# Which engine issues the store DMAs of an adaLN transformer block on one core

## The chip, the cores and the metric

One of the eight cores of a Trainium2 chip runs the whole program, in float32. The metric is device time in microseconds, the median of several executions. Beside it there is the profile of one execution of the same program, with every instruction's start, duration and what ended the idle time before it.

## What is computed

The input is four sequences of 1024 tokens of 512 features. A small product gives six modulation vectors for each sequence; the two gates are kept at least 0.25 in size.

```python
mod = (_silu(L0_c) @ L0_wmod).reshape(L0_c.shape[0], 6, 1, -1)
sa, ca, ga, sb, cb, gb = (mod[:, 0], ..., mod[:, 5])
h = _layernorm(x) * (1 + ca) + sa
x = x + ga * attn(h)      # 16 query heads of 32, one key and value head, causal, softmax, output product
h = _layernorm(x) * (1 + cb) + sb
x = x + gb * ffn(h)       # Hadamard transform, up and gate 512 -> 2048, silu(gate) * up,
                          # Hadamard transform, down 2048 -> 512
```

## The kernel before, in words

**Tiling.** The 4096 tokens are eight blocks of 512 (`order`), each of two halves of 256 columns or four tiles of 128 rows. For each block there is attention (scores, row minima, exponentials, scales, transposes, the product with the values), then the feed-forward part: for each of 16 chunks of 128 hidden features the products of gate and up (`gate_up`, products at L1076, arranged so that 14 small products and some sums replace 16), and the products with the transformed down weights (`down`, L1214). Attention of later blocks is mixed on TensorE with the feed-forward part of earlier ones.

**Who sets the order.** The instructions are not written in the order in which they run. Some thirty generators (`ranked`, L1257) yield `Op`s, each with an engine, an estimated cost, the keys that it reads and writes, and the code that emits it. `Flow` (L47) keeps an estimated time for each engine and for the transfers, and emits next the operation that could begin first; among those of the same engine within `SLACK` the stream's rank decides. Each engine then runs its own instructions strictly in the emitted order, and waits, where it must, at the head of its queue. An operation with another engine or cost can therefore change the order everywhere.

**The DMAs.** All of them come from `load` (L288), which makes an operation of SP with a cost of 0.5 us for the planner. SP's queue holds 1270 of them. The ones that matter here:
- `wd<-wd_d` (L1048): a row of the down weights, into a ring of three buffers, once per down step. `wg`, `wu` (L1018): weights of gate and up, rings of two and three. GpSimd mixes them into three sums, four operations for each chunk (`mixes`, L1040).
- `o_d<-oT` (L659): a half of the attention's rows of a tile. ScalarE copies it from PSUM to `oT` in four copies (L640), the store takes it to DRAM, and four loads bring back its quarters in another arrangement (L661), which GpSimd adds up (L663, L664). Then comes the output product of attention. The first block doesn't take this way, so there are 56 such stores, of 512 KB each.
- `x2_d<-xr` (L720; the profile names this tensor x_d): a tile of the residual after attention. GpSimd adds the attention's part to `xr` (L715, L717), the store follows, and VectorE (statistics at L304) and GpSimd (L310, L311) prepare the second normalization. Then `xr` is overwritten in place: by L315 in the first block, and in the later ones by VectorE's L746 and L748, eighteen GpSimd operations of the Hadamard transform (L754), a transpose, and four small stores `xTf_d<-xr`. The loads `bt<-xTf_d` (L772) bring the result back turned, as the right-hand operand of gate and up. There are 32 stores of `x2_d`; `xo<-x2_d` (L1235) reads them much later.
- `out<-xo` (L1250): a tile of the output. VectorE scales the down product (L1243), GpSimd adds the residual (L1248), the store follows. There are 32.

**Semaphores of DMAs.** Eight semaphores are given to the DMAs in turn, and a DMA that gets one waits for the DMA before it on that semaphore, unless this is known to be done.

Of the kernel before, what the change touches and what calls it, by code (L numbers as in the profile page):

```python
# [19 lines left out]
P = 128  # L20
# [141 lines left out]
def adaln_block(ctx, tc, x_d, small_d, const_d, wmod_d, qwT_d, kwT_d, vwT_d, vb_d, owT_d, ob_d,  # L162
                wdp_d, wupT_d, wgT_d, wdT_d, out_d):
    nc = tc.nc
# [15 lines left out]
    x2_d = dram.tile([B * S, D], F32, name="x2_d")  # L180
# [3 lines left out]
    o_d = dram.tile([2, P, 4, HB], F32, name="o_d")  # L184
# [15 lines left out]
    def token(n):  # L200

        b, t = order[n // NT]
        return b * S + t * TB + n % NT * P

    def new_batch(i):
        return i == 0 or order[i][0] != order[i - 1][0]
# [78 lines left out]
    def until(queue, name):  # L285
        return lambda: bool(queue) or name in over

    def load(mb, dst, src, writes, reads=()):  # L288
        return Op("SP", 0.5, lambda: nc.sync.dma_start(dst, src), reads, writes, mb=mb)  # L289

    def bk(b):
        return ("bank", b)
# [9 lines left out]
    def stats_op(which, n, x, dst, keys, key):  # L302
        def emit():
            nc.vector.bn_stats(bn[which][:, n % 2, :], x)  # L304
            nc.vector.bn_aggr(dst, bn[which][:, n % 2, :])
        return Op("DVE", 0.85, emit, keys, [key])

    def rstd_op(dst, src, keys, key):
        def emit():
            nc.gpsimd.tensor_scalar_add(dst, src, EPS)  # L310
            nc.gpsimd.tensor_tensor(dst, dst, mhalf[:, 0:dst.shape[-1]], ALU.pow)  # L311
        return Op("POOL", 1.0, emit, keys, [key])

    def norm_op(x, xk, m, rs, rkey):
        return Op("DVE", 0.62, lambda: nc.vector.tensor_scalar(x, x, m, rs, ALU.subtract, ALU.mult), [rkey], [xk])  # L315

    def turn(which, n, x, xk):


        hh, j = divmod(n, 2)  # L320
        dst = xT_d[which][hh].rearrange("(b q) (j a i) -> j a q b i", q=32, j=2, a=4)[j]
        for a, r in enumerate(rows):
            yield load(0.0625, dst[a], x[r, :].rearrange("q (b i) -> q b i", i=32), [("xT", which, n, a)], [xk])

    def turned_back(which, hh, c, dst, key):

        return load(0.25, dst, xT_d[which][hh][c * P:(c + 2) * P, :].rearrange("(c p) n -> p c n", p=P), [key],
                    [("xT", which, n, a) for n in (2 * hh, 2 * hh + 1) for a in range(4)])
# [23 lines left out]
    def first_norms(halves):  # L352
        for hh in halves:
# [5 lines left out]
            for j in range(2):  # L359
                r = token(2 * hh + j)  # L360
                yield load(0.25, x[:, j, :], x_d[r:r + P, :], [(xk, j)])
# [288 lines left out]
    def exchange():  # L650


        while True:
            yield until(to_exchange, "attend")
            if not to_exchange:
                break
            i, ql, half = to_exchange.popleft()
            o, key = oT[:, half], ("oT", half)
            yield load(0.5, o_d[half], o, [("o_d", half)], [key])  # L659
            for j, r in enumerate(rows):  # L660
                yield load(0.125, o[r], o_d[half].rearrange("(c d) j x -> j d c x", c=4)[j], [key], [("o_d", half)])  # L661
            o = o.rearrange("p c x -> p (c x)")
            yield Op("POOL", 1.3, lambda: nc.gpsimd.tensor_add(o[:, 0:512], o[:, 0:512], o[:, 512:1024]), [], [key])  # L663
            yield Op("POOL", 0.77, lambda: nc.gpsimd.tensor_add(  # L664
                aT[:, 2 * half:2 * half + 2, :].rearrange("p c q -> p (c q)"), o[:, 0:HB], o[:, HB:512]), [key], ["aT"])
            st.folded += 1
            to_finish.append((i, ql, half))
        over["exchange"] = True
# [36 lines left out]
    def add():  # L705

        for i in range(NBLK):
            if new_batch(i):
                yield load(0.25, obga, gates_d[2, order[i][0], :].partition_broadcast(P), ["obga"], [("gates", 2)])
            for ql in range(NT):  # L710
                j, n = ql % 2, i * NT + ql
                x, xk, r = xr[:, j, :], ("xr", j), n * P
                yield lambda: st.turned > n - 2
                yield load(0.25, x, x_d[token(n):token(n) + P, :], [xk])
                yield Op("POOL", 1.3, lambda: nc.gpsimd.tensor_add(x, x, obga), ["obga"], [xk])  # L715
                yield lambda: bool(to_add)
                yield Op("POOL", 1.3, lambda: nc.gpsimd.tensor_add(x, x, y), ["y"], [xk])  # L717
                to_add.popleft()
                st.y_held = False
                yield load(0.25, x2_d[r:r + P, :], x, [("x2", n)], [xk])  # L720
                m, rs = mv["f"][:, j, :], rstd["f"][:, j, 0:1]
                yield stats_op("f", n, x, m, [xk], ("mvf", j))
                yield rstd_op(rs, m[:, 1:2], [("mvf", j)], ("rstdf", j))
                if i >= ROWS:
                    to_fwht.append((n, m, rs))
                    continue
                yield norm_op(x, xk, m[:, 0:1], rs, ("rstdf", j))
                st.added = n + 1
# [496 lines left out]
    def outputs():  # L1225
        for hh in range(NHALF):
            i, hf = divmod(hh, 2)
            if hh == 0:
                yield lambda: st.prepared
            if hf == 0 and new_batch(i):  # L1230
                yield load(0.25, ff["gb"], gates_d[1, order[i][0], :].partition_broadcast(P), ["gb"], [("gates", 1)])
            yield lambda: st.normed > i
            for j in range(2):
                n = 2 * hh + j
                yield load(0.25, xo[:, j, :], x2_d[n * P:(n + 1) * P, :], [("xo", j)], [("x2", n)])  # L1235
            yield lambda: bool(to_out)
            _, acc = to_out[0]
            for j in range(2):
                n = 2 * hh + j
                x, xk = xo[:, j, :], ("xo", j)  # L1240
                yield lambda: not st.y_held
                st.y_held = True
                yield Op("DVE", 0.7, lambda: nc.vector.tensor_mul(y, ps[:, acc[j], :], ff["gb"]),  # L1243
                         [bk(acc[j]), "gb"], ["y"])
                banks.give(acc[j])
                if j == 1:
                    to_out.popleft()
                yield Op("POOL", 1.3, lambda: nc.gpsimd.tensor_add(x, x, y), ["y"], [xk])  # L1248
                st.y_held = False
                yield load(0.25, out_d[token(n):token(n) + P, :], x, [("out", n)], [xk])  # L1250


    def early(rank, later):
# [3 lines left out]
    ranked = [  # L1257
        (early(-5.073, -12.067), copies), (early(0.821, 4.686), sums), (early(8.123, -0.319), multiply),
        (early(2.934, -0.393), outputs), (early(6.498, 6.37), load_weights_once), (early(-6.572, -10.863), load_jobs),
        (early(2.446, -2.829), mods), (early(5.09, -0.692), attend), (early(-1.32, 5.096), finish),  # L1260
        (early(0.121, 5.957), exchange), (early(-13.435, 16.471), add), (early(-5.268, 7.992), transformed),
        (early(5.174, 6.804), minima), (early(6.312, -0.74), scores), (early(-13.598, 4.773), second_norms),
        (early(-0.125, 3.627), lambda: first_norms([0])), (early(-5.211, 13.107), lambda: first_norms([1])),
# [60 lines left out]
```

## Time and profile before

| | |
|---|---|
| median of 3 runs | 2028.36 us (2024.61 to 2028.71) |
| the profiled execution, its own time | 2024.31 us |
| its span, first to last instruction | 2022.5 us |
| mean granted clock of TensorE | 0.989 |
| busy on ScalarE, VectorE, GpSimd | 1125.0, 1375.3, 1047.9 us |
| issue to landing, median: o_d<-oT, x_d<-xr, out<-xo | 3.8, 3.1, 2.2 us |

The profile's page lists each engine's busy time (PE is TensorE, PEld its weight loads, DVE VectorE, ACT ScalarE, POOL GpSimd; SP only issues), the chain of work that ended last, the costliest groups of instructions and the DMA issues. A view of the waits gives, for each engine and line, what the wait was for, with the total in us, the number of waits and the longest one. A view by time gives start and duration of each instruction, with the idle time before it and its releaser in brackets. "SPq" is SP's queue: a row there is a DMA's issue, and a wait there holds up all DMAs behind it.

### The profile page before, as it was taken

To read this page: it belongs to the slowest core of one execution; us is meant where nothing else is said; L and a number is where in the kernel's file an instruction comes from. 1 tells how busy PE (TensorE), PEld (TensorE's weight loads), DVE (VectorE), ACT (ScalarE), POOL (GpSimd) and SP (SyncE) were. 2 spreads that over 40 slices of the span, in tenths; PEclk is the share of its full clock that TensorE was granted. 3 is DMA by queue.
4 is the path that set the end of the run, shared out by engine and by line. 5 is a ranking of instruction groups with operands and counts; after the bars stand their busy time and mean duration, and the time that the engine had idled before them with its cause. 6 is when DMAs were issued, how large, how long until landed. Compare 5 with 4: busy or idle time off the path is not lost.

```text
span 2022.5 us, 41770 instructions
## 1 busy us (share of the span) xinstructions
PE 1947.4 (96%) x15656; PEld 1258.1 (62%) x15656; DVE 1375.3 (68%) x3139; ACT 1125.0 (56%) x2371; POOL 1047.9 (52%) x1374
## 2 busy tenths in 40 slices
PE   7898999999999999999999999999999999999998
PEld 5556666556674666746676566663666646674774
DVE  4886778788757667878748688776567768642441
ACT  5677755685557554766546575576455676510220
POOL 2762467636564486447453356444567435662440
PEclk9999999999999999999999999999899999999999
DMA  7433555654347645465345634357554444345333
GB/s 233 135 111 105 161 159 134 184 156 122 107 131 210 178 137 153 136 187 141 103 129 141 199 116 120 101 152 212 149 156 121 131 146 138 104 122 180 107 103 115
DMA packets 387394, 289.42 MB, mean 143 GB/s; under 512 B 129508, under 2 KB 319076, under 8 KB 387192
## 3 DMA queue, kind: packets, MB, share of 16 engines
q1 hardware_dynamic: 387192, 286.75, 49.4%
q8 instruction: 124, 2.03, 0.4%
q14 instruction: 78, 0.64, 0.1%
HBM read 222.67 MB, written 64.00 MB: 142 GB/s over the span
## 4 chain that ended last, share of the span: by engine, by line
PE 85%; DMA 5%; POOL 3%; DVE 3%; issue 3%; SPq 1%; ACT 0%; POOLq 0%; DVEq 0%; ACTq 0%
PE ps L1076 38%; PE ps L1214 19%; PE ps L299 11%; PE ps L626 8%; PE ps L502 7%; DMA wd<-wd_d 2%; SPq L289 1%; DMA xTf_d<-xr 1%; POOL ws L1040 1%; DVE p L526 1%; POOL u L754 1%; DMA wg<-in_wgT 1%; PE ps L984 0%; DMA oT<-o_d 0%; POOL xr L754 0%
## 5 line engine op out<-in xcount | busy, mean ns | idle before, releaser
L1214 PE MATMUL ps<-wd,g 128*128 128x512 f32 x1024 | 485.4, 608 | 24.8 <-DMA wd<-wd_d 19.6
L549 ACT ACTIVATE p<-p,nm 128x512 f32<-128x512 f32 (+7 forms) x512 | 391.2, 768 | 78.5 <-DVE nm L526 78.3
L1076 PE MATMUL ps<-bt,ws 128*128 128x256 f32 x1536 | 380.6, 384 | 5.5 <-DVE bt L807 3.5
L583 ACT ACTIVATE p<-p,rden 128x640 f32<-128x640 f32 (+7 forms) x480 | 347.6, 784 | 46.1 <-DVE rden L563 45.9
L598 DVE STREAM_TRANSPOSE p<-p 128x512 f32<-128x512 f32 (+7 forms) x256 | 342.6, 1359 | 20.8 <-ACT p L583 19.1
L1214 PEld LDWEIGHTS ps<-wd,g 128*128 128x128 f32 x1024 | 187.4, 191 | 256.6 <-issue 189.6
L1076 PEld LDWEIGHTS ps<-bt,ws 128*128 128x128 f32 x1536 | 291.5, 192 | 61.1 <-issue 8.7
L526 DVE CUSTOM_DVE_ANT_0 p<-ps,maskw 128x512 f32<-128x512 f32 (+3 forms) x512 | 279.8, 581 | 53.8 <-PE ps L502 53.6
L1163 DVE TENSOR_TENSOR s<-ps,s 128x256 f32<-128x256 f32 x384 | 160.1, 419 | 198.5 <-PE ps L1076 149.9
L1076 PE MATMUL ps<-bt,wu 128*128 128x256 f32 x1024 | 269.9, 386 | 0.0
L1040 POOL TENSOR_TENSOR ws<-wu 128x256 f32<-128x256 f32 x128 | 105.3, 822 | 285.1 <-DMA wu<-in_wupT 258.3
L1076 PE MATMUL ps<-bt,wg 128*128 128x256 f32 x1024 | 251.2, 383 | 0.9 <-DVE nm L526 0.7
L1076 PEld LDWEIGHTS ps<-bt,wu 128*128 128x128 f32 x1024 | 188.9, 190 | 91.0 <-issue 39.6
L1076 PEld LDWEIGHTS ps<-bt,wg 128*128 128x128 f32 x1024 | 195.0, 192 | 52.4 <-issue 18.2
L626 PE MATMUL ps<-p,vrep 32*32 32x256 f32 (+1 forms) x8256 | 197.3, 410 | 14.7 <-issue 11.5
L754 POOL TENSOR_TENSOR u<-xr 128x256 f32<-128x256 f32 x280 | 171.6, 631 | 48.1 <-DVE xr L748 40.4
L1154 ACT COPY s<-ps 128x256 f32<-128x256 f32 x128 | 47.8, 373 | 245.0 <-PE ps L1076 244.9
L502 PE MATMUL ps<-kT,qT 32*128 32x512 f32 (+3 forms) x1536 | 174.7, 528 | 2.0 <-DVE nm L526 1.2
L1179 ACT ACTIVATE th<-s,wgh 128x512 f32<-128x512 f32 x128 | 92.5, 722 | 147.4 <-DVE s L1163 145.6
L626 PEld LDWEIGHTS ps<-p,vrep 32*32 32x32 f32 x8256 | 120.0, 103 | 85.2 <-issue 38.9
L1040 POOL TENSOR_TENSOR ws<-ws,wg 128x256 f32<-128x256 f32 x128 | 99.7, 779 | 137.0 <-DMA wg<-in_wgT 123.2
L640 ACT COPY oT<-ps 128x256 f32<-128x256 f32 x256 | 78.4, 386 | 126.1 <-PE ps L626 62.7
(118 smaller groups left out, 2317.2 us busy)
## 6 DMA issues: line engine op xcount, KB each, us to landing
wd<-wd_d SPq DMA_DIRECT2D x256, 256.0 KB, 2.9
wg<-in_wgT SPq DMA_DIRECT2D x128, 256.0 KB, 3.5
wu<-in_wupT SPq DMA_DIRECT2D x128, 256.0 KB, 2.8
o_d<-oT SPq DMA_DIRECT2D x56, 512.0 KB, 3.8
oT<-o_d SPq DMA_DIRECT2D x224, 128.0 KB, 3.2
xr<-in_x SPq DMA_DIRECT2D x32, 256.0 KB, 3.4
x_d<-xr SPq DMA_DIRECT2D x32, 256.0 KB, 3.1
xo<-x_d SPq DMA_DIRECT2D x32, 256.0 KB, 3.6
```

The source lines that it names most:

```text
L299: nc.tensor.matmul(out, l, r, start=(k == 0), stop=(k == len(pairs) - 1))
L502: nc.tensor.matmul(ps[:, bb[j], m * n:(m + 1) * n], qT[r, c, u.ql % 2 * P:(u.ql % 2 + 1) * P], kT[r, u.kv[kb] * TB:u.kv[kb] * TB + n], sta ...
L526: yield Op("DVE", 0.245 + 0.00103 * n, lambda: nc.vector.tensor_tensor_reduce(o, ps[:, bb[j], k * n:(k + 1) * n], m, -1.0, nm[:, slot, 0, ...
L549: yield Op("ACT", act_cost(u.kmax) + 0.19, lambda: nc.scalar.activation(e, e, AF.Exp, bias=nm[:, slot, u.t, j:j + 1], scale=-1.0, accum_ou ...
L583: yield Op("ACT", act_cost(u.kmax), lambda: nc.scalar.activation(e, e, AF.Copy, scale=r), [("rden", ds, c)], [u.key(h)])
L598: yield Op("DVE", 0.135 + 0.00105 * 2 * u.kmax, lambda: nc.vector.transpose(e, e), [], [u.key(h), u.key(h + 1)])
L626: nc.tensor.matmul(ps[rows[c], bb[g], 0:w], vrep[rows[g], v0 + c, :], pv[rows[g], :, k:k + 32], start=(kt == 0), stop=(kt == nkt - 1))
L754: yield Op("POOL", 0.66, lambda: getattr(nc.gpsimd, "tensor_" + fn)(w[:, h:h + D // 2], pairs[:, 0, :], pairs[:, 1, :]), [], [xk, "u2"])
L1040: yield Op("POOL", 0.78, lambda: getattr(nc.gpsimd, "tensor_" + e)(a[o][0], a[x][0], a[y][0]), [a[n][1] for n in (x, y) if n != "A21" or o ...
L1076: nc.tensor.matmul(o, w[:, c, :], bt[:, t, c, :], start=start and c == 0, stop=stop and c == 1, skip_group_check=True)
L1163: yield Op("DVE", 0.43, lambda: nc.vector.tensor_add(s[:, j, :], ps[:, bank, half * HB:(half + 1) * HB], s[:, j, :]), [bk(bank)], [sk[j]])
L1214: nc.tensor.matmul(ps[:, acc[j], :], g[:, j * P:(j + 1) * P], ff["wd"][:, m % NWD, :], start=(f == 0), stop=(f == NFC - 1))
```

## The change

`load` is given the issuing engine, SP unless told otherwise. Three stores get another one, the engine that writes the data just before: `o_d<-oT` goes to ScalarE, `x2_d<-xr` and `out<-xo` to GpSimd. The loads stay on SP, and so do the stores `xTa_d`, `xTf_d`, `wd_d` and `gates_d`. The planner counts 0.5 us on the new engine. Lines behind L288 move down by one.

```diff
-    def load(mb, dst, src, writes, reads=()):
-        return Op("SP", 0.5, lambda: nc.sync.dma_start(dst, src), reads, writes, mb=mb)
+    def load(mb, dst, src, writes, reads=(), eng="SP"):
+        issuer = {"SP": nc.sync, "ACT": nc.scalar, "POOL": nc.gpsimd}[eng]
+        return Op(eng, 0.5, lambda: issuer.dma_start(dst, src), reads, writes, mb=mb)
...
             o, key = oT[:, half], ("oT", half)
-            yield load(0.5, o_d[half], o, [("o_d", half)], [key])
+            yield load(0.5, o_d[half], o, [("o_d", half)], [key], "ACT")
...
                 st.y_held = False
-                yield load(0.25, x2_d[r:r + P, :], x, [("x2", n)], [xk])
+                yield load(0.25, x2_d[r:r + P, :], x, [("x2", n)], [xk], "POOL")
...
                 st.y_held = False
-                yield load(0.25, out_d[token(n):token(n) + P, :], x, [("out", n)], [xk])
+                yield load(0.25, out_d[token(n):token(n) + P, :], x, [("out", n)], [xk], "POOL")
```

## The prediction

> **What bounds the kernel now.** I read the page first, then the waits of TensorE, the waits of SP's own queue, and last the timeline of the largest stall that both point to.
>
> ```profile
> span 2022.5 us, 41770 instructions
> PE 1947.4 (96%) x15656; PEld 1258.1 (62%) x15656; DVE 1375.3 (68%) x3139; ACT 1125.0 (56%) x2371; POOL 1047.9 (52%) x1374
> PE 85%; DMA 5%; POOL 3%; DVE 3%; issue 3%; SPq 1%; ACT 0%; POOLq 0%; DVEq 0%; ACTq 0%
> ```
>
> TensorE is the bound: 75 us of the span are not matmul, and no change of issuers removes matmul time. A table by stage (windows) splits the 75: 26 in the first 180 us, about 42 from 180 to 1850, nothing to 1984, 7 in the tail. A gain can come only out of these.
>
> ```profile
> PE ps L1214 <- DMA wd<-wd_d: 19.6, 10, 4.4
> PE ps L626 <- issue: 11.5, 20, 1.1
> PE ps L880 <- DMA raw<-in_wmod: 6.6, 1, 6.6
> PE ps L1214 <- DVE g L1189: 5.2, 9, 0.6
> ```
>
> Of what TensorE waits for, only the first row (us, times, longest) runs through SP: the ring of three down-weight rows.
>
> ```profile
> SPq L289 <- PE ps L1214: 486.9, 223, 9.6
> SPq L289 <- PE ps L1076: 414.8, 204, 10.6
> SPq L289 <- ACT oT L640: 89.1, 20, 8.8
> SPq L289 <- POOL xr L717: 66.9, 15, 16.7
> SPq L289 <- DMA o_d<-oT: 49.0, 25, 5.1
> ...
> SPq L289 <- POOL xo L1248: 39.6, 24, 6.3
> ```
>
> SP mostly waits for TensorE to free weight buffers, which costs nothing. The three moved stores hold it for 89.1 + 66.9 + 39.6 = 196 us. Where that reaches TensorE:
>
> ```profile
> 370.27 0.33 SPq L289 DMA_DIRECT2D x_d<-xr  x1
> 372.35 0.34 SPq L289 DMA_DIRECT2D out<-xo  x1
> 372.78 1.35 SPq L289 DMA_DIRECT2D wd<-wd_d  x3
> ...
> 375.59 1.98 PE L1214 MATMUL ps<-wd,g 128*128 128x512 f32 x4 [3.40 <-DMA wd<-wd_d]
> ```
>
> Three weight loads stand behind two stores that wait for GpSimd's adds, and TensorE stops 3.40 us.
>
> **What is removed from SP.** 120 issues (56 + 32 + 32) at 0.34 to 0.38 us, 44 us, and the 196 us of waiting. The Trainium skill speaks against a gain: "DMA: Bandwidth & Descriptors", section "Issuing engines are not separate DMA queues", says that several issuers save only the sequencer's time to start a DMA. By that rule the gain is the 44 us of an SP that waits over 900 us for TensorE: zero. The rows add what the rule leaves out, in-order blocking, so I count it where TensorE sat idle. The stall above, 3.4 us, goes. Of the other 16.2 us of that row, the timeline shows the two longest (650.8 and 894.9, 4.3 and 4.4 us) behind "bt<-xTf_d" loads that wait for a landing; those stay. The one near 1835 (3.9 us) is a wd load that took 5.5 us to land; no store was waiting in front of it. Gain between 0 and 8 us; I take 4, the proven stall and a little. Much of the 89.1 us doesn't go at all: the quarter loads oT<-o_d stay on SP and must wait for the landing of the same store (49.0 us already), and the order of the programs has only 2.7 SP entries (2.8 after) between a store and its first quarter load. What is late next there is that landing.
>
> **What is added to ScalarE.** 56 issues at 0.38 us, plus an estimated 0.3 us for its own last oT copy to finish: 38 us on an engine idle for 900. It often waits for TensorE anyway (s L1154: 244.9 us, 119 of 128 times). Behind a store in its queue stand exps and the s copies that TensorE's next product needs; if that cover were gone all 38 would show. I take 2, ends 0 and 8.
>
> **A wait that is new.** The built order shows semaphores: 55 of the 56 ScalarE stores also wait on a DMA semaphore, one of eight that all SP and ScalarE DMAs share in turn; for 54 of them the DMA before it on that semaphore is SP's, the eighth before the store. So ScalarE, with exps and s copies behind it, can wait for SP. In the trace SP was the early one: it waited for oT copies 20 times. Stores that follow their copies at once were issued 0 to 2.5 us after the copies ended; eight DMAs back is 8 x 2022/1270 = 13 us earlier on average, and a landing takes about 3. So nothing is to be waited for in most cases, and SP will run further ahead. But weight loads wait for TensorE up to 10.6 us, and a burst of loads after one leaves no margin. Ends: 0, and 10 stores x 8 us, of which TensorE sees half, 40. I take 3, near the zero that the trace speaks for.
>
> **What is added to GpSimd.** 64 stores. No row shows GpSimd issuing a DMA. Nearest rows: an issue on SP, 0.34 us, and a 512-column add on GpSimd, 1.27 us. I take 1.0 each, 64 us on an engine idle for 975 us and waiting 258.3 + 123.2 us for weight loads before its mixes. It shows only where GpSimd's chain sets the end: four x2 stores of the first block (the chain there runs xr L717, p L580, tmp L963, rstdf L310 and L311 from 94.9 to 102.6; TensorE idles 4.1 us at 162 for the normalized row), +3; the 18 GpSimd adds and subtracts per row at later block starts (idle near 1407 to 1424, 5 us), +2; the last output, whose add ends at 2019.5, 3.0 us before the end, +1. Sum +6, ends 0 (at SP's price) and 16.
> The skill has a darker rule: "SBUF — State Buffer", section "SBUF: two separate sides", warns that a DMA issued from GpSimd is starved of descriptors while VectorE holds the shared port, 620 ns becoming about 3100. That would be 2.5 us a store, 160 us on GpSimd, and put this item and the next at their upper ends, +26 together. The trace shows the lock seldom: the add L717 takes 1264/1275/2241 ns min/median/max beside a VectorE that is 68% busy. I follow the row.
>
> **A later landing.** VectorE overwrites xr in place (L746, L315) and waits for the x2 store to have left; now 3.5 us in three waits. If the store lands 0.7 to 1.5 us later, up to 32 x 1 us falls on VectorE, with minima and sums queued behind it. A quarter reaching TensorE: I take 3, ends 0 and 10.
>
> **The order of everything else.** The planner sees other engine loads and reorders. Matmuls, vector and scalar operations are the same set; on TensorE the order first differs at instruction 360 of 7854. Changes between whole-array, row and tile matmuls number 424 before and 420 after. Down steps with under 6 us of matmul since the ring slot was freed: 79 before, 82 after, with 143 and 122 other SP entries ahead of their loads. So the order is as good as before by these counts; 0, ends -8 and +8.
>
> **Sum.** -4 + 2 + 3 + 6 + 3 + 0 = +10 us on the profiled execution's 2024.3 (span 2022.5, 1.8 around it). The median of the runs, 2028.36, is 4 above that execution; I add the 10 there: 2038.
>
> **Rivals.** A measurement tells about 0.2%, 4 us, from no change.
> 1. The sum, costs on GpSimd and ScalarE over a small gain: 2033 to 2054, likeliest 2038. Chance 0.52.
> 2. Faster: with 122 for 143 entries in front of tight weight loads, and none that waits for GpSimd, half of the 19.6 us goes, -9, and GpSimd's issues hide under its 381 us of waiting for weights: about 2020 (2014 to 2024). It decides once a GpSimd store costs no more than SP's 0.34 us, which takes the two GpSimd items from 9 to about 2. For it: the stall at 372; against: the other long stalls aren't behind stores. 0.22.
> 3. It doesn't free SP: the wait for oT reappears as the wait for the store's landing in front of the quarter loads (49 us becoming 120 or more), and GpSimd's price is hidden: 2025 to 2032. 0.14.
> 4. ScalarE waits for SP's semaphore at some ten stores: +40, 2068 (2055 to 2085). 0.12.
> The range 2018 to 2062 leaves out the low end of case 2 and most of case 4. Case 1 alone has 2033 to 2054. Faster 0.22, same 0.14, slower 0.64.
>
> **What would show it.** Right: SP's waits for oT L640, xr L717 and xo L1248 gone, those for DMA o_d<-oT grown; GpSimd rows for stores near 1 us; TensorE's wait for wd under 19.6 us; more idle on TensorE before 180 us; VectorE waits for DMA x_d<-xr above 3.5 us. The semaphore price is wrong if ScalarE rows show waits for SP's DMAs of over 20 us in all. I am wrong altogether if stores on GpSimd cost under 0.4 us (then case 2), or over 2 us (then past 2050).

## The result, and the profile after

The changed kernel takes 2053.48 us (median of 4 runs, 2050.98 to 2059.28) against 2026.48 us for the kernel before beside it: a ratio of 1.0141, 95% interval 1.0111 to 1.0172, so 27 us slower. The forecast was 10 us slower. The profiled execution took 2053.11 us, at nearly the clock of before (0.987 for 0.989).

From the page of the changed kernel: span, busy times and the chain that ended last; from the view of its groups, the two of GpSimd's stores. The groups' columns are busy us and mean ns of one, then the idle time just before.

```profile
span 2051.3 us, 41831 instructions
PE 1958.0 (95%) x15656; PEld 1256.9 (61%) x15656; DVE 1383.2 (67%) x3139; ACT 1125.2 (55%) x2371; POOL 1091.0 (53%) x1438
PE 80%; DMA 6%; issue 4%; POOL 4%; DVE 4%; SPq 1%; ACT 0%; POOLq 0%; DVEq 0%; ACTq 0%
...
L290 POOL DMA_DIRECT2D x_d<-xr x32 | 19.9, 623 | 8.6 <-POOL xr L718 8.6
L290 POOL DMA_DIRECT2D out<-xo x32 | 18.4, 577 | 9.5 <-POOL xo L1249 9.2 <-DMA oT<-o_d 0.3
```

The span grew by 28.8 us. Of that, 10.6 are in the busy row of TensorE (1947.4 to 1958.0, with the same 15656 matmuls; the lower clock alone would make about 4, an estimate from 1947.4 x 0.989/0.987) and 18.2 are idle (75.1 to 93.3). The two groups answer what no row of before could: a store costs GpSimd 0.58 to 0.62 us, and in nearly every case another 0.3 us of waiting for its own add to finish.

The waits of TensorE after (us in total, times, longest):

```profile
PE ps L1215 <- DMA wd<-wd_d: 18.5, 14, 5.1
PE ps L627 <- issue: 14.4, 19, 1.7
PE ps L1215 <- DVE g L1190: 10.8, 16, 2.3
PE ps L881 <- DMA raw<-in_wmod: 6.6, 1, 6.6
PE ps L300 <- ACT aT L687: 3.7, 1, 3.7
```

The wait that the change could have shortened, for down weights, is as long as before (18.5 us for 19.6). The stall at 372 us is gone, and others of the kind stand elsewhere. What grew is spread: 5.6 us more for VectorE's gated product g, 2.9 us in the row "issue", 3.7 us for ScalarE's aT. No new row is near 18 us.

The waits of SP's queue after:

```profile
SPq L290 <- PE ps L1215: 520.9, 220, 9.4
SPq L290 <- PE ps L1077: 477.3, 221, 10.1
SPq L290 <- DVE xr L758: 68.3, 21, 12.8
SPq L290 <- DMA o_d<-oT: 63.9, 21, 10.2
SPq L290 <- DMA out<-xo: 61.4, 25, 6.1
```

And one row of before:

```profile
SPq L289 <- DMA out<-xo: 18.6, 13, 3.3
```

SP no longer waits for xr and xo, and for oT only 8.0 us in three waits. Two things take their place: the wait for the landing of o_d (49.0 to 63.9 us), which the forecast named, and the wait for the landing of out<-xo (18.6 to 61.4 us), which it didn't. The second one stands before the load of the next tile into the same buffer xo. Before, SP waited for xo twice, 39.6 us for the add and 18.6 for the landing, 58.2 together; it now waits 61.4 in one place, so for this store nothing is set free at all. Most of the rest of the time set free is waiting for TensorE: the first two rows hold 998 us, before 902.

The end of the program by time (start, duration, in brackets the idle time before), first before, then after:

```profile
2018.24 1.26 POOL L1248 TENSOR_TENSOR xo<-xo,y 128x512 f32<-128x512 f32 x1 [0.80 <-DVE y L1243]
2019.53 0.34 SPq L289 DMA_DIRECT2D out<-xo  x1
```

```profile
2043.14 1.27 POOL L1249 TENSOR_TENSOR xo<-xo,y 128x512 f32<-128x512 f32 x1
2044.71 0.56 POOL L290 DMA_DIRECT2D out<-xo  x1 [0.30 <-POOL xo L1249]
```

The last add ends at 2044.4 and the span at 2051.3, 6.9 us later. Before, the last add ended at 2019.5 and the span at 2022.5, 3.0 later. So 3.9 us of the loss lie in the tail. The remaining 25 build up gradually over blocks.

### The profile page after: what moved, and what is told of

Read it like the earlier page. It is cut to its first block, busy times and chain, and to the rows that moved or that the text cites. A ratio compares the mean times of both kernels' runs of the same rounds, so it can differ in the third digit from the quotient of the medians.

```text
span 2051.3 us, 41831 instructions
## 1 busy us (share of the span) xinstructions
PE 1958.0 (95%) x15656; PEld 1256.9 (61%) x15656; DVE 1383.2 (67%) x3139; ACT 1125.2 (55%) x2371; POOL 1091.0 (53%) x1438
## 4 chain that ended last, share of the span: by engine, by line
PE 80%; DMA 6%; issue 4%; POOL 4%; DVE 4%; SPq 1%; ACT 0%; POOLq 0%; DVEq 0%; ACTq 0%
PE ps L1077 36%; PE ps L1215 18%; PE ps L300 11%; PE ps L627 8%; PE ps L503 6%; DMA wd<-wd_d 2%; DMA xTf_d<-xr 1%; SPq L290 1%; DVE p L599 1%; POOL ws L1041 1%; POOL u L755 1%; DVE p L527 1%; POOL xr L755 1%; PE ps L985 1%; PE ps L988 0%
## 5 line engine op out<-in xcount | busy, mean ns | idle before, releaser
L1215 PE MATMUL ps<-wd,g 128*128 128x512 f32 x1024 | 490.0, 612 | 29.5 <-DMA wd<-wd_d 18.5
L527 DVE CUSTOM_DVE_ANT_0 p<-ps,maskw 128x512 f32<-128x512 f32 (+3 forms) x512 | 278.7, 582 | 59.3 <-PE ps L503 58.2
L1151 ACT COPY s<-ps 128x512 f32<-128x512 f32 x128 | 74.8, 584 | 129.8 <-PE ps L1077 122.4
```

The source lines that it names most:

```text
L527: yield Op("DVE", 0.245 + 0.00103 * n, lambda: nc.vector.tensor_tensor_reduce(o, ps[:, bb[j], k * n:(k + 1) * n], m, -1.0, nm[:, slot, 0, ...
L1215: nc.tensor.matmul(ps[:, acc[j], :], g[:, j * P:(j + 1) * P], ff["wd"][:, m % NWD, :], start=(f == 0), stop=(f == NFC - 1))
```

## The experiments

The change does two things at once: another engine executes three stores, and the planner, told so, emits everything in another order. The theories are: the loss is the issuers' (A; as the forecast had it, mostly GpSimd's); the loss is the order's (B); or both add to it. Ratios are against the kernel before on the same chip, with 95% intervals. The median of before there was 2029.15 us for the first four kernels, 2025.16 for the last one, and 2028.6 to 2030.0 for the others.

### Issuers alone, order alone

In the first kernel the planner still counts SP for these stores, so that TensorE and VectorE have the order of before; only the issuing engines change.

```diff
-        return Op(eng, 0.5, lambda: issuer.dma_start(dst, src), reads, writes, mb=mb)
+        return Op("SP", 0.5, lambda: issuer.dma_start(dst, src), reads, writes, mb=mb)
```

> The planner is told SP for all stores, as before, so that every engine's other instructions stand in the order of before; only the issuing engines are those of the change. Theory A (the new issuers cost the time: GpSimd's and ScalarE's issues, SP waiting for landings of GpSimd's stores): about +25 us over before, 2045 to 2055. Theory B (the planner's new order costs it, the issuers only the tail): +4 to +8 us, 2028 to 2036.

In the second the planner counts the new engines, and SP issues all.

```diff
-        issuer = {"SP": nc.sync, "ACT": nc.scalar, "POOL": nc.gpsimd}[eng]
+        issuer = nc.sync
```

> The planner is told ScalarE and GpSimd, so that the order is that of the change, but SP issues every DMA. Theory A: within 5 us of before. Theory B: +20 us or more, 2045 to 2055. If both e1 and e2 are slower by about half, the two add up.

Measured: issuers alone 2041.56 us, 1.0061 (1.0039 to 1.0084); order alone 2045.99 us, 1.0082 (1.0058 to 1.0106). The product is 1.0144, the whole change 1.0141. Both are real, for neither interval holds 1, and they add. The order of the emitted program, which the forecast put at 0, is the larger one by the medians, 16.6 us against 12.4; the two intervals overlap, so that which is larger isn't settled.

### Which issuer

Issuers alone again, in the order of before, split by engine.

```diff
-        issuer = {"SP": nc.sync, "ACT": nc.scalar, "POOL": nc.gpsimd}[eng]
+        issuer = {"SP": nc.sync, "ACT": nc.scalar, "POOL": nc.sync}[eng]
```

> Order of before; only the 56 stores of attention's rows go to ScalarE. Theory A with ScalarE's semaphore as the cause: +15 us or more, and ScalarE rows that wait for SP's DMAs. Theory A with GpSimd as the cause: within 4 us of before. Theory B: within 4 us.

```diff
-        issuer = {"SP": nc.sync, "ACT": nc.scalar, "POOL": nc.gpsimd}[eng]
+        issuer = {"SP": nc.sync, "ACT": nc.sync, "POOL": nc.gpsimd}[eng]
```

> Order of before; only the 64 stores of x2 and of the output go to GpSimd, with 0.56 to 0.64 us for each issue as in the profile of the changed kernel. Theory A with GpSimd as the cause: +20 us. Theory B: +4 to +8 us, of which some 4 in the tail (last add to end 6.9 us for 3.0).

Measured: ScalarE alone 2031.48 us, 1.0010 (0.9996 to 1.0023); GpSimd alone 2040.64 us, 1.0058 (1.0037 to 1.0079). The issuers' loss is GpSimd's. ScalarE's 56 stores cost nothing that can be told from zero, but they gain nothing either. The waits of SP's queue with ScalarE alone show why:

```profile
SPq L290 <- DMA o_d<-oT: 70.9, 22, 10.3
SPq L290 <- POOL xr L718: 68.9, 16, 16.5
SPq L290 <- POOL xo L1249: 39.3, 25, 6.1
```

Of the 89.1 us for oT 8.6 are left, and the wait for the store's landing has gone from 49.0 to 70.9: the quarter loads still need those data. And with GpSimd alone, in the same view:

```profile
SPq L290 <- ACT oT L641: 101.0, 23, 10.3
SPq L290 <- DMA out<-xo: 68.5, 22, 6.7
```

The wait for out's landing grows with the order of before too (18.6 to 68.5), so it belongs to the GpSimd store and not to the planner. It is 10 us more than the 58.2 that SP spent on xo before.

### What GpSimd's share is made of

One store at a time, in the order of before (`load` as in the first kernel, so that the planner counts SP): first only x2, then only the outputs.

```diff
-                yield load(0.25, x2_d[r:r + P, :], x, [("x2", n)], [xk])
+                yield load(0.25, x2_d[r:r + P, :], x, [("x2", n)], [xk], "POOL")
```

> Order of before; only the 32 x2 stores go to GpSimd. If the first block's chain and the later landing in front of VectorE cost it: +4 to +7 us, seen before 200 us. If the output stores cost it (tail, and SP waiting for their landing in front of the xo loads): 0 to +4 us.

```diff
-                yield load(0.25, out_d[token(n):token(n) + P, :], x, [("out", n)], [xk])
+                yield load(0.25, out_d[token(n):token(n) + P, :], x, [("out", n)], [xk], "POOL")
```

> Order of before; only the 32 output stores go to GpSimd. At least +4 us, all of it after the last matmul. If SP's wait for the landing in front of the xo loads (68.5 us in the profile with both, 18.6 before) reaches TensorE: +8 to +10 us and SP's rows show about 65 us for DMA out<-xo again.

Measured: x2 2033.84 us, 1.0031 (1.0018 to 1.0045); out 2033.90 us, 1.0027 (1.0012 to 1.0043). Together 1.0058, as measured for both. So neither store alone is the culprit.

In the view by stages (TensorE's busy time, its matmuls and granted clock, then the share and rate of the DMAs), x2 alone shows where its price arises. First before, then x2 on GpSimd:

```profile
0.00:180.00 180.00, 154.06 (x1389) 0.96 0.51 152
0.00:180.00 180.00, 151.14 (x1366) 0.94 0.50 145
```

With x2 on GpSimd, TensorE has begun 23 matmuls fewer by 180 us and been busy 2.9 us less. All four x2 stores of the first block fall into this stretch. In the order of before, the kernels without x2 stores on GpSimd have begun 1388 or 1389 matmuls by then (before, ScalarE alone, outputs alone), those with them 1366 to 1379 (x2 alone, GpSimd alone, issuers alone). So a part of the price of x2 arises in the first block, where the forecast looked for it.

The next kernel leaves all stores with SP and holds GpSimd beside each x2 and out store, which pass `beside`, with a one-column power on scratch of 0.57 us in the mean, about as long as an issue. The scratch takes no part in the result.

```diff
-        return Op("SP", 0.5, lambda: nc.sync.dma_start(dst, src), reads, writes, mb=mb)
+        def emit():
+            nc.sync.dma_start(dst, src)
+            if beside:
+                nc.gpsimd.tensor_tensor(idle1, idle1, mhalf[:, 0:1], ALU.pow)
+        return Op("SP", 0.5, emit, reads, writes, mb=mb)
```

> Order of before, every store on SP; beside each x2 and output store GpSimd gets a one-column power operation of 0.59 us on a scratch tile, as long as its DMA issue (38 us in all). If the time that GpSimd is held is the price: +5 to +12 us. If landing and waits are: within 2 us of before.

Measured: 2031.47 us, 1.0015 (1.0000 to 1.0030), with GpSimd busy 1084.7 us, 37 more than before. Holding the engine costs some 3 us, a quarter of GpSimd's 11.8 and at most about half, and here too TensorE has begun fewer matmuls by 180 us (1377, busy 151.42 us). The stores hold GpSimd somewhat longer, 38.5 us of issues and 13.6 of waiting for the adds (GpSimd alone), so that in proportion the hold would cost 4 us, an estimate. A second part is the tail, seen with the outputs alone on GpSimd and, for comparison, with x2 alone. By time, outputs on GpSimd:

```profile
2023.28 1.27 POOL L1249 TENSOR_TENSOR xo<-xo,y 128x512 f32<-128x512 f32 x1
2024.85 0.56 POOL L290 DMA_DIRECT2D out<-xo  x1 [0.30 <-POOL xo L1249]
```

x2 on GpSimd, outputs on SP:

```profile
2023.82 1.26 POOL L1249 TENSOR_TENSOR xo<-xo,y 128x512 f32<-128x512 f32 x1 [0.80 <-DVE y L1244]
```

The spans are 2029.3 and 2028.6 us, so the last add is followed by 4.8 us in the first and 3.5 in the second. In the kernels with both stores on GpSimd it is 6.9 (issuers alone, GpSimd alone, the whole change). So the tail gives 2 to 4 us. What is left of GpSimd's share, some 4 to 6 us, may lie in the later landings (with GpSimd alone, of out 3.2 us in the median for 2.2, with SP's loads into xo behind them, and of x2 3.9 for 3.1), but no run isolates it: that part stays open.

### What the order is worth

The order is split likewise, SP issuing everything (`load` as in the second kernel): the planner is told ScalarE for o_d alone, or GpSimd for x2 and the outputs alone.

```diff
-            yield load(0.5, o_d[half], o, [("o_d", half)], [key])
+            yield load(0.5, o_d[half], o, [("o_d", half)], [key], "ACT")
```

> SP issues everything; the planner is told ScalarE for the attention's rows alone. If the order's 16.8 us come from planning ScalarE with 56 stores: +15 us, and e8 near 0. If any other order costs: +8 to +25 us here and in e8 alike, not adding up to 16.8.

```diff
-                yield load(0.25, x2_d[r:r + P, :], x, [("x2", n)], [xk])
+                yield load(0.25, x2_d[r:r + P, :], x, [("x2", n)], [xk], "POOL")
...
-                yield load(0.25, out_d[token(n):token(n) + P, :], x, [("out", n)], [xk])
+                yield load(0.25, out_d[token(n):token(n) + P, :], x, [("out", n)], [xk], "POOL")
```

> SP issues everything; the planner is told GpSimd for the x2 and output stores alone. If the order's 16.8 us come from planning GpSimd with 64 stores: +15 us, and e7 near 0. If any other order costs: +8 to +25 us here and in e7 alike.

Measured: told ScalarE 2052.79 us, 1.0112 (1.0087 to 1.0137); told GpSimd 2023.64 us, 0.9978 (0.9964 to 0.9992), which is faster than both kernels. The two ratios multiply to 1.0090, near the 1.0082 of both together. Waits of TensorE, told ScalarE:

```profile
PE ps L1215 <- DMA wd<-wd_d: 13.6, 10, 3.9
PE ps L627 <- issue: 12.7, 15, 1.6
PE ps L1215 <- DVE g L1190: 8.9, 14, 1.6
...
PE ps L503 <- DVE y L1244: 5.4, 2, 3.7
PE ps L627 <- DVE p L599: 4.6, 5, 3.0
PE ps L1077 <- DVE bt L808: 4.5, 3, 1.8
PE ps L339 <- DVE nm L527: 4.2, 1, 4.2
PE ps L1077 <- DVE nm L527: 4.0, 3, 2.3
```

Before, the rows with VectorE that answer to these:

```profile
PE ps L338 <- DVE nm L526: 4.1, 1, 4.1
PE ps L1076 <- DVE bt L807: 3.5, 2, 1.8
PE ps L626 <- DVE p L598: 0.9, 2, 0.7
PE ps L1076 <- DVE nm L526: 0.7, 1, 0.7
```

Told GpSimd:

```profile
PE ps L627 <- issue: 11.0, 13, 1.6
PE ps L1215 <- DVE g L1190: 9.2, 15, 1.0
PE ps L881 <- DMA raw<-in_wmod: 6.7, 1, 6.7
PE ps L1215 <- DMA wd<-wd_d: 6.1, 8, 1.7
```

The slowest order waits 13.6 us for down weights, less than the kernel before (19.6). Most of its additional idle time stands in rows in which TensorE waits for VectorE: the five behind the dots hold 22.7 us, for 9.2 before. The fastest order does save in the row for down weights, 13.5 us, and gives some of it back elsewhere.

To see whether that says something of these engines or only of orders, two kernels change nothing but the planner's cost of every SP operation, from 0.5 to 0.52 and to 0.48 us.

```diff
-        return Op("SP", 0.5, lambda: nc.sync.dma_start(dst, src), reads, writes, mb=mb)
+        return Op("SP", 0.52, lambda: nc.sync.dma_start(dst, src), reads, writes, mb=mb)
```

> The kernel before with the planner's cost of a DMA at 0.52 us in place of 0.5, every DMA on SP: another order without any other purpose. If any other order costs as much as that of the change did (16.8 us): +8 to +25 us. If the order of the change is bad for its own reason (ScalarE and GpSimd planned with stores): within 6 us of before.

> The kernel before with the planner's cost of a DMA at 0.48 us, every DMA on SP. A second order without purpose: if any other order costs, +8 to +25 us; if not, within 6 us of before.

Measured: 0.52 gives 2033.5 us, 1.0023 (1.0013 to 1.0034); 0.48 gives 2042.26 us, 1.0064 (1.0039 to 1.0089). The first is within the 6 us that were expected if other orders cost nothing of their own, the second, 12.3 us, is not. So an order that nobody aimed at can move the time by three quarters of what the change's order does. But neither reaches the 22.8 us of the planner told ScalarE, and its ratio and that of GpSimd give the whole: that it is bad in itself to plan ScalarE with these stores isn't excluded by two other orders. With the time of the profiled execution split into matmul and the rest:

| order (SP issues all stores) | ratio | span us | TensorE busy | span less busy | granted clock |
|---|---|---|---|---|---|
| planner told GpSimd for x2, out | 0.9978 | 2021.1 | 1948.7 | 72.4 | 0.990 |
| before | 1 | 2022.5 | 1947.4 | 75.1 | 0.989 |
| SP cost 0.52 | 1.0023 | 2031.2 | 1954.0 | 77.2 | 0.989 |
| SP cost 0.48 | 1.0064 | 2037.8 | 1955.4 | 82.4 | 0.985 |
| the change's order | 1.0082 | 2043.2 | 1955.4 | 87.8 | 0.988 |
| planner told ScalarE for o_d | 1.0112 | 2052.0 | 1960.2 | 91.8 | 0.984 |

Of five other orders one is better than that of before, four are worse, and TensorE's idle time grows with the loss. Its busy time mostly grows too, but in two rows the clock alone would make most of that: 1947.4 us at 0.989 are 1955.3 at 0.985 and 1957.3 at 0.984, an estimate. The clock of these two is lower in all their executions taken together (0.985 in the mean of six each, 0.988 in the 27 of before beside them). Among those 27, a clock lower by 0.001 goes with about 1.8 us more, so that some 6 to 7 us of either loss would go with the clock, an estimate. In the other orders the means differ from before by 0.001 or less. Whether an order itself lowers the clock no run shows.

### Do they add in the good order too?

The change's GpSimd part alone, order and issuers both; o_d stays wholly with SP.

```diff
-            yield load(0.5, o_d[half], o, [("o_d", half)], [key], "ACT")
+            yield load(0.5, o_d[half], o, [("o_d", half)], [key])
```

> The GpSimd part of the change alone, order and issuers both: the planner is told GpSimd for the stores of x2 and of the outputs and GpSimd issues them; o_d<-oT stays wholly with SP. If order and issuers add, as they did for the whole change (1.0061 x 1.0082 = 1.0144 against 1.0141), this is e8's order (0.9978) times e4's issuers (1.0058): 1.0036, near 2036 us. Rival: the price of GpSimd's issues was one of the order in which it was measured; then the good order hides it and the time stays near e8's, 0.998 (2024 us), or the order loses its gain once GpSimd's stores land late, and the time is that of the issuers alone or more, 1.006 to 1.010 (2041 to 2049 us).

Measured: 2032.3 us, 1.0037 (1.0023 to 1.0051), where adding says 1.0036. So GpSimd's stores cost 0.6% here (1.0037 against 0.9978) as in the order of before; in the order of the whole change the issuers, ScalarE's included, cost the same (1.0141 against 1.0082). A good order doesn't hide them.

## Why the prediction was right in direction and too small

The direction was right, and the reason for it half: the forecast had a loss at the GpSimd stores, which is there, and none in the order, where at least as much is lost by the medians. That 2053 lies in the 2033 to 2054 of case 1 is luck: the room there was left for GpSimd's stores and their landings, and it was the order that filled it.

**The order of everything else, forecast 0 (ends -8 and +8), measured +16.6.** This is the term that was mis-sized, and its upper end was too low by half. The step that failed is the inference "the order is as good as before by these counts". The counts were of changes between matmul kinds and of down steps with a tight weight ring; none was of what VectorE has ready when TensorE needs it. The slowest order of all waits less for down weights than before, and loses where TensorE waits for VectorE. The 75 us in which TensorE does no matmul can grow as well as shrink, and the order of before is a good one: four of five others are worse. Why one order is worse than another stays open. No single row ranks them, and the span less busy time in the table only restates the loss.

**GpSimd's stores, forecast +6 and +3 for later landings, measured +11.8.** Right in kind, a quarter short. The issue was taken at 1.0 us and is 0.58 to 0.62, with the 0.3 us of waiting 0.88 in all: 64 stores hold GpSimd 56 us for the 64 forecast. A hold without a store, 37 us in all, costs some 3 us (0 to 6), for which the three places where GpSimd's chain shows (3 + 2 + 1) were not too low. Of the three, the first block's +3 can be seen where x2 alone or the hold alone is added (2.9 and 2.6 us less matmul before 180 us). In the changed kernel, with its other order, this sign, more idle time on TensorE before 180 us, is nearly missing: 153.69 us of matmul for 154.06. The last output was taken at +1 and is +3.9 in the changed kernel, and that SP would wait for out's landing in front of the xo loads, 61.4 us, was not seen: the forecast counted the 39.6 us for the add as set free. VectorE's wait for x2's landing went from 3.5 to 5.5 us; before, then after:

```profile
DVE xr L746 <- DMA x_d<-xr: 2.8, 1, 2.8
DVE xr L315 <- DMA x_d<-xr: 0.7, 2, 0.5
DVE xr L747 <- DMA x_d<-xr: 4.5, 4, 2.4
DVE xr L316 <- DMA x_d<-xr: 1.0, 2, 0.8
```

The threshold "wrong altogether under 0.4 us" was not reached. The starvation of GpSimd's DMAs that the Trainium skill warns of ("SBUF — State Buffer", section "SBUF: two separate sides"), which the forecast put at some 2.5 us a store from the page's figures, an estimate, is not seen at that size: in the changed kernel no issue took longer than 0.77 us, and from issue to landing the medians are 2.9 us for x2 (3.1 before) and 3.7 for out (2.2 before). Whether VectorE held the shared port during any of these stores, and whether that has a part in out's 1.5 us, no run shows.

**ScalarE's stores, forecast +2, and its wait on shared semaphores, +3; measured +2 together (-1 to +5), with whatever SP gains by it.** The issue is 0.33 us. The fourth rival falls. Waits of ScalarE for DMAs after:

```profile
ACT oT L641 <- DMA xTa_d<-xn: 11.0, 1, 11.0
ACT hT L378 <- DMA hT<-xTa_d: 9.5, 4, 5.1
...
ACT oT L641 <- DMA o_d<-oT: 2.4, 1, 2.4
```

In front of the oT copies there are 13.4 us, in two waits, under the 20 set as the mark; with ScalarE alone in the order of before there are none. So being earlier by about eight DMAs was margin enough, as the forecast argued.

**SP set free, forecast -4, measured no gain.** With ScalarE alone SP is rid of 80 us of waiting for oT and the time doesn't fall. In the order of before, TensorE's wait for down weights is 23.1 us with ScalarE's stores moved, 15.1 with GpSimd's and 20.9 with all three, for 19.6. With all three the stall of 3.40 us is gone, but at the next product of attention TensorE waits where it did not before:

```profile
380.62 3.38 PE L627 MATMUL ps<-p,vrep 32*32 32x256 f32 x160 [2.12 <-DVE p L599]
```

So VectorE's transposes were next in line, and most of what the stall gave back was lost to them there (2.3 us with GpSimd's stores alone). Here the third rival was right: the wait for oT returns as a wait for the landing. The rule of the Trainium skill ("DMA: Bandwidth & Descriptors", section "Issuing engines are not separate DMA queues"), that several issuers save only the sequencer's time, fits better than the gain of 4 us taken from the stall. The second rival, faster, got one thing right unawares: an order in which the row for down weights is short exists (6.1 us), but it came with SP issuing everything.

## What to carry to other kernels

Where a planner emits the program, an edit of an engine or a cost is two edits: run the new order with the old issuers and the old order with the new issuers before a cause is named, and give the order a spread of its own in the forecast (here -0.2% to +1.1% over five orders, most of them worse). Moving a store to the engine that makes the data takes a wait out of one queue only to leave it with whoever needs the landing: look for the loads that reread the stored data, and for those that refill the buffer. The version that beats both kernels leaves every store with SP and only tells the planner that GpSimd pays for x2 and out (2023.64 us, 0.9978); that is one good draw among six orders, not a rule.

## What the runs showed of the hardware that was not expected

After the data of the last store issued by GpSimd have moved, more than 4 us pass before the program ends. The DMA's busy tenths in the changed kernel from 2044 to 2053 us, 40 slices of 0.225 us, and in the kernel before, with SP's store, from 2018 to 2024 us, 40 slices of 0.15 us:

```profile
DMA  9400000099910000000000000000000000000000
DMA  0089996000000002999940000000000000000000
```

In the first the store's data have moved by 2046.7 us, 2.0 us after the issue began, and the span ends at 2051.3. In the second they have moved by about 2021.1, and the span ends at 2022.5. So 4.6 us stand against 1.4. With only the outputs on GpSimd, in the order of before, the whole stretch from the last add took 4.8 us instead of the 6.9 with x2's stores on GpSimd as well; why is open.
